# Two float32r products in place of one float32 product for a softmax's sums over partitions

## The chip, the cores and the metric

The kernel runs on one NeuronCore of a Trainium2 chip. The time is the device time of one execution in microseconds (us), taken as the median of several executions. The engines are named as in the profile: PE (TensorE, matrix products; PEld is its loading of the stationary operand), DVE (VectorE), ACT (ScalarE), POOL (GpSimd) and SP (SyncE, which here issues DMAs). They run beside each other, each works through its own queue in order, and they wait for each other by semaphores.

## The reference, cut to what matters

Two attention layers run over eight images of 32 x 32 tokens with 512 channels, each with a group norm before it and a residual after it. The first has 16 heads of 32 channels, the second 4 heads of 128 channels and a relative position term. The second layer's softmax is where the change is:

```
xn     = group_norm(x)
q, k, v = xn @ Wq * scale, xn @ Wk, xn @ Wv        # 4 heads of 128
scores = q @ k + position(q)                       # 1024 x 1024 per head
attn   = exp(scores) / sum over keys of exp(scores)
x      = x + (attn @ v) @ Wo
```

The whole computation is in float32.

## The kernel before, in words

Everything is kept transposed: channels or keys lie on the 128 partitions, tokens along the free dimension. Softmax is taken without subtracting a maximum; a second, general path (which does not run with these inputs) exists for the case that a sum grows too large, so the reciprocals of all sums are put into a tile `checks`.

Each image goes through: load and first norm (`load`), projections of the first layer (`before_0`), first attention (`attention_0`), its output projection (`after_0`), second norm (`norm_1`), projections of the second layer (`second`), second attention (`attention_1`), output projection and store (`after_1`). The function `side_by_side` walks through the steps of one image's `attention_0` and puts beside them pieces of the other parts of the images before and after it, by an account of costs. The projections use seven products where eight would be needed by the plain rule (`seven`, `by_columns` at L299: four products of 32 columns each, side by side in the array).

The steps of `attention_1` have cost 0 in this account, so all 64 of an image come in one unbroken run between two steps of the first attention. I call such a run a burst; there are eight, one per image. In six of them a first attention of a later image still waits to go on.

A burst walks over 4 heads x 2 halves of the queries (a block) x 8 blocks of keys (a step j). A step has

- `front`: two products into one PSUM bank, `ps` = keys x queries in float32 (L631, called QK below) plus the position term in float32r (L632, called pos), and the exponential `e` on ACT (L634);
- `back`, one step behind: the product of the values with `e` into the accumulator `acc` (L643, called AV or acc), and the addition of `e` to `esum` on DVE (L652 for the first pair, L654 for the rest). In the last step of a block ACT copies `acc` out (L657).

After step 1 of the next block comes `finish` for the block that ended: the sum of `esum` over the partitions, as one float32 product with a 128 x 128 matrix of ones (L663, into `su`, in the trace `sums`), and `normalise`: a copy by ACT (L482), a transpose (L484), a reciprocal (L487), the entry in `checks` (L490), a transpose back (L500), all on DVE, and a product with the output on POOL (L504).

Buffers come in rotation by their tags. The PSUM banks have three buffers, which `ps`, `acc` and the sums of the second attention share with the projections and the position term:

```
def bank(name, shape=None):
    return psum.tile(shape or [P, NB], F32, tag="bank", name=name, bufs=3)
```

The tag `e1` has three buffers of 128 x 512 (the exponentials `e`), `es1` two (`esum`), and `rec` two (the copy of the sums and its transpose, for both layers).

The first attention is like the second one with four heads of 32 channels at once: L516 is four products that each use 32 rows of the array (QK0), L524 one exponential of 128 x 2048, L535 four products that each use 32 columns (AV0), L544 and L546 the additions, L556 its sums. In the trace L282 is the last step of a norm (four per image, 128 x 1024 each) and L694 and L240 the load's transposes and statistics; in a burst these belong to a coming image.

The order of instructions on each engine isn't that of the source: a scheduler sets it when the program is built, with a model of its own of how long each instruction takes, and lets an instruction of later work go first where it believes that the engine would wait. Waits are semaphores between engines.

## Time and profile before

| | |
|---|---|
| time, median of 3 | 3999.2 us (3998.8 to 4000.18) |
| profiled execution, span | 3997.9 us |
| busy PE, DVE, ACT, POOL | 3830.9, 2534.3, 1723.6, 579.0 us |
| L663: records, union of busy time | 128 (64 products, two records each), 65.4 us |
| L643, L631, L632: union of busy time | 521.9, 523.6, 406.7 us |

A row of the view in order of time gives the start in us from the span's start, the length, the engine, the line, the operation, what it writes and reads, shape and type, and the number of merged records; in brackets stands the idle time of the engine before it and what ended it. One float32 product gives two records on PE. Records of PE overlap, since a product's record begins before the array is free for it[...]. What a product holds of the array is therefore read from the distance between starts.

### The profile page before, as it was taken

The numbers are of one execution on the slowest core, as the hardware profiler recorded it, in microseconds if no ns is written. First come the engines' busy times: TensorE is split into PE (matmuls) and PEld (weight loads), VectorE is DVE, ScalarE is ACT, GpSimd is POOL, SyncE is SP. The second block draws the span as 40 slices with busy tenths as digits, with TensorE's granted clock in tenths as the row PEclk, the third lists the DMA queues.
The fourth block names the chain that finished last, engine by engine and source line by source line (L and its number), as shares of the span: only waits on it lengthen the run. The fifth ranks groups of instructions, "written<-read, shape, count | busy, mean of one in ns | idle before, by whom it ended". The sixth has DMA issues, their size and how long they took to land. (4 is left out here: it accounts for less than half of the span.)

```text
span 3997.9 us, 71625 instructions
## 1 busy us (share of the span) xinstructions
PE 3830.9 (96%) x30338; PEld 1418.1 (35%) x30338; DVE 2534.3 (63%) x2915; ACT 1723.6 (43%) x1761; POOL 579.0 (14%) x396
## 2 busy tenths in 40 slices
PE   6898999998999989999999989999899998999998
PEld 3232244232443324432244323433234332244353
DVE  5776675576655767458674686646866468664544
ACT  1454453444434444344443445434454444543132
POOL 1340101121111201012100121001110112111101
PEclk9999999999999999999999999999999999999999
DMA  5320120141201512015120241203311032110401
GB/s 145 120 86 25 50 63 6 38 115 58 62 6 38 129 51 60 4 40 143 37 54 12 75 99 38 53 19 93 81 40 45 26 93 60 37 63 10 126 19 22
DMA packets 498694, 234.18 MB, mean 59 GB/s; under 512 B 286368, under 2 KB 478144, under 8 KB 497344
## 3 DMA queue, kind: packets, MB, share of 16 engines
q1 hardware_dynamic: 495232, 214.79, 20.1%
q0 software_dynamic: 2608, 13.70, 0.9%
q8 instruction: 241, 3.95, 0.4%
q10 hardware_dynamic: 528, 1.05, 0.1%
q14 instruction: 85, 0.70, 0.1%
HBM read 170.72 MB, written 58.72 MB: 57 GB/s over the span
## 5 line engine op out<-in xcount | busy, mean ns | idle before, releaser
L524 ACT ACTIVATE e<-ps 128x2048 f32<-128x2048 f32 x512 | 962.0, 1879 | 878.5 <-PE ps L516 723.4
L546 DVE TENSOR_TENSOR es<-es,e 128x2048 f32<-128x2048 f32 x384 | 903.4, 2352 | 450.9 <-ACT e L524 448.0
L516 PE MATMUL ps<-q,k 32*128 32x512 f32 x4096 | 608.0, 649 | 97.3 <-ACT e L524 97.1
L634 ACT ACTIVATE e<-ps 128x512 f32<-128x512 f32 x512 | 305.9, 598 | 583.1 <-PE ps L632 553.0
L535 PE MATMUL acc<-e,v 128*32 128x512 f32 x4096 | 553.9, 613 | 1.4 <-ACT e L524 1.0
L631 PE MATMUL ps<-q,k 128*128 128x512 f32 x1024 | 523.6, 593 | 0.3 <-DVE posT L617 0.3
L643 PE MATMUL acc<-e,v 128*128 128x512 f32 x1024 | 521.9, 592 | 0.0
L654 DVE TENSOR_TENSOR es<-es,e 128x512 f32<-128x512 f32 x384 | 286.9, 747 | 267.1 <-ACT e L634 266.3
L632 PE MATMUL ps<-posT,sel 128*128 128x512 f32 x512 | 406.7, 794 | 0.0
L504 POOL TENSOR_TENSOR q<-q,su 128x512 f32<-128x512 f32 x128 | 201.0, 1571 | 1397.7 <-DVE su L500 1349.6
L516 PEld LDWEIGHTS ps<-q,k 32*128 32x128 f32 x4096 | 165.6, 185 | 500.1 <-issue 250.5
L631 PEld LDWEIGHTS ps<-q,k 128*128 128x128 f32 x1024 | 193.6, 190 | 246.5 <-issue 240.2
L643 PEld LDWEIGHTS acc<-e,v 128*128 128x128 f32 x1024 | 193.1, 189 | 146.8 <-issue 105.2
L535 PEld LDWEIGHTS acc<-e,v 128*32 128x32 f32 x4096 | 81.9, 108 | 394.1 <-issue 348.0
L544 DVE TENSOR_TENSOR es<-e,e 128x2048 f32<-128x2048 f32 x64 | 172.3, 2692 | 36.1 <-ACT e L524 36.1
L484 DVE STREAM_TRANSPOSE tu<-su 128x512 f32<-128x512 f32 x128 | 90.7, 709 | 114.4 <-ACT su L482 114.1
L482 ACT COPY su<-sums 128x512 f32<-128x512 f32 x128 | 75.1, 586 | 171.1 <-PE sums L556 103.3
L632 PEld LDWEIGHTS ps<-posT,sel 128*128 128x128 f32 x512 | 97.3, 190 | 122.5 <-issue 122.5
L652 DVE TENSOR_TENSOR es<-e,e 128x512 f32<-128x512 f32 x64 | 44.9, 701 | 145.5 <-ACT e L634 145.5
L617 DVE TENSOR_TENSOR posT<-pp,posT 32x512 fp32r<-32x512 f32 x128 | 111.7, 873 | 31.7 <-ACT posT L612 30.4
L612 ACT CAST posT<-pp 32x512 fp32r<-32x512 f32 x128 | 105.6, 825 | 46.1 <-PE pp L599 38.0
L408 POOL TENSOR_TENSOR v<-b_v,p_v 128x512 f32<-128x512 f32 x32 | 55.8, 1744 | 479.1 <-ACT p_v L373 458.5
(188 smaller groups left out, 4409.3 us busy)
## 6 DMA issues: line engine op xcount, KB each, us to landing
w_qkv<-ws_qkv SPq DMA_DIRECT2D x168, 128.0 KB, 2.5
xs<-in_x SPq DMA_DIRECT2D x256, 64.0 KB, 2.6
d<-x0T SPq DMA_DIRECT2D x32, 512.0 KB, 3.0
x1T<-d SPq DMA_DIRECT2D x32, 512.0 KB, 6.3
d<-x1T SPq DMA_DIRECT2D x32, 512.0 KB, 3.6
x2T<-d SPq DMA_DIRECT2D x32, 512.0 KB, 6.0
out<-ot SPq DMA_DIRECT2D x256, 64.0 KB, 2.0
w_qkv<-in_L_conv_w_qkv SPq DMA_DIRECT2D x126, 128.0 KB, 2.2
```

What stands on the lines that cost most here:

```text
L504: nc.gpsimd.tensor_tensor(dst, dst, su, op=ALU.mult)
L516: nc.tensor.matmul(ps[:, r, :], k[m][rows, j * P : (j + 1) * P], q[m][rows, h * NB : (h + 1) * NB], start=True, stop=True,)
L524: nc.scalar.activation(e, ps, AF.Exp, scale=D0 ** -0.5)
L535: nc.tensor.matmul(acc[r * D0 : (r + 1) * D0, :], v[:, j, c0 : c0 + D0], e[:, r, :], start=(j == 0), stop=(j == NT - 1),)
L544: nc.vector.tensor_add(state["esum"], state["first"], e)
L546: nc.vector.tensor_add(state["esum"], state["esum"], e)
L617: nc.vector.tensor_sub(rest, logits, greater)
L631: nc.tensor.matmul(ps, k[h][:, keys], q[:, h, queries], start=True, stop=False)
L632: nc.tensor.matmul(ps, sel[:, keys], posT[:, h, queries], start=False, stop=True)
L634: nc.scalar.activation(e, ps, AF.Exp, scale=1.0 / math.sqrt(D1))
L643: nc.tensor.matmul(acc, v[:, j, h * D1 : (h + 1) * D1], e, start=(j == 0), stop=(j == NT - 1),)
L654: nc.vector.tensor_add(state["esum"], state["esum"], e)
```

## The change

The sum over the partitions is no longer one float32 product. `esum` is copied by ACT into a float32r tile (`greater`, in the trace `sg`), which rounds it; DVE subtracts that from `esum` and writes what is left, also as float32r (`rest`, in the trace `sr`). Two float32r products with the ones add both into the same bank. The rest keeps what the rounding takes away, so that the sum stays nearly as exact as in float32, while each product is of the cheaper kind. `greater` takes its buffer from the tag of the exponentials, `rest` from that of the sums' copies. The ones become a float32r tile that is read as float32 elsewhere.

```diff
-    ones = consts.tile([P, P], F32, tag="ones", name="ones")
-    nc.gpsimd.memset(ones, 1.0)
+    ones_r = consts.tile([P, P], F32R, tag="ones", name="ones")
+    nc.gpsimd.memset(ones_r.bitcast(F32), 1.0)
+    ones = ones_r.bitcast(F32)
...
         def finish(h, c, esum):
             name = f"1_{b}_{h}_{c}"
             su = bank(f"sums_{name}")
-            nc.tensor.matmul(su, ones, esum, start=True, stop=True)
+
+            greater = mem.tile([P, NB], F32R, tag="e1", name=f"sg_{name}", bufs=3)
+            nc.scalar.copy(greater, esum)
+            rest = mem.tile([P, NB], F32R, tag="rec", name=f"sr_{name}", bufs=2)
+            nc.vector.tensor_sub(rest, esum, greater.bitcast(F32))
+            nc.tensor.matmul(su, ones_r, greater, start=True, stop=False)
+            nc.tensor.matmul(su, ones_r, rest, start=False, stop=True)
             normalise(q[:, h, c * NB : (c + 1) * NB], su, name)
```

## The prediction

> **What bounds the kernel now.** I read the page's first two parts, then the windows of the second layer's attention, then its instructions in order of time.

> ```profile
> PE 3830.9 (96%) x30338; PEld 1418.1 (35%) x30338; DVE 2534.3 (63%) x2915; ACT 1723.6 (43%) x1761; POOL 579.0 (14%) x396
> PEclk9999999999999999999999999999999999999999
> ```

> TensorE (PE) is busy 96% of the time at full clock. Busy includes pipelining, so I ask where it is really gapless.

> ```profile
> 2057.00:2173.00 116.00, 116.00 (x303) 55.64 (x305) 61.17 (x108) 42.45 (x72) 12.05 (x9) 1.00 0.02 9
> 2173.00:2380.00 207.00, 206.00 (x2010) 63.05 (x2002) 143.21 (x143) 93.60 (x75) 35.62 (x24) 1.00 0.33 86
> ```

> The columns are length, then busy time of PE, PEld, DVE, ACT, POOL. The first window is one "burst", the second layer's attention for one image, eight of which are in the kernel. PE never rests in it, nor in the 207 us after it. So here one us of PE work, or of PE waiting, is one us of the result. The change sits at the end of each of a burst's eight blocks (4 heads, 2 query halves). One such end on each engine:

> ```profile
> 2140.78 1.02 PE L643 MATMUL acc<-e,v 128*128 128x512 f32 x2
> 2141.64 1.02 PE L663 MATMUL sums<-es,ones 128*128 128x512 f32 x2
> 2142.49 1.02 PE L631 MATMUL ps<-q,k 128*128 128x512 f32 x2
> 2142.95 0.80 PE L632 MATMUL ps<-posT,sel 128*128 128x512 f32 x1
> 2143.59 1.02 PE L643 MATMUL acc<-e,v 128*128 128x512 f32 x2
> 2144.44 1.02 PE L631 MATMUL ps<-q,k 128*128 128x512 f32 x2
> ...
> 2140.98 0.60 ACT L634 ACTIVATE e<-ps 128x512 f32<-128x512 f32 x1 [0.50 <-PE ps L632]
> 2142.75 0.59 ACT L482 COPY su<-sums 128x512 f32<-128x512 f32 x1 [1.18 <-PE sums L663]
> 2143.78 0.60 ACT L634 ACTIVATE e<-ps 128x512 f32<-128x512 f32 x1 [0.45 <-PE ps L632]
> ...
> 2141.61 0.69 DVE L652 TENSOR_TENSOR es<-e,e 128x512 f32<-128x512 f32 x1 [3.20 <-ACT e L634]
> 2143.44 0.71 DVE L484 STREAM_TRANSPOSE tu<-su 128x512 f32<-128x512 f32 x1 [1.14 <-ACT su L482]
> ```

> Slots come from starts, not durations. L643 to L663 is 0.86, L663 to L631 0.85: a full float32 product holds the array 0.86 us. L631 to L643, with the float32r product L632 between, is 1.10, so float32r costs 1.10 - 0.86 = 0.24. The su copy (L482) starts 0.26 after the sums' slot ends, an exponential 0.19 after L632's slot ends. Call 2140.78 time 0: before, the third score product (query-key product of key block 3, "QK3") starts at 3.66.

> [...]L299 (32 columns) to L516 (32 rows) takes 1.83 instead of 1.71, and L516 holds 1.07 instead of 0.86:

> ```profile
> 2174.26 1.90 PE L299 MATMUL y_q<-f_xn,w_qkv 128*32 128x512 f32 x16
> 2176.09 1.14 PE L516 MATMUL ps<-q,k 32*128 32x512 f32 x8
> 2177.16 1.07 PE L535 MATMUL acc<-e,v 128*32 128x512 f32 x8
> ```

> [...]

> **Part 1, the product itself.** 64 times, 0.86 becomes 2 x 0.24 = 0.48: -0.38 each, -24 us if nothing waits.

> **Part 2, the copy and the subtraction.** 64 ACT copies (0.59, the row L482) and 64 DVE subtractions (0.69, the row L652). Neither engine is full, so their time as such is free. What matters is where they stand. The changed program's order at an ordinary end is:

> ```
> PE:  acc0, acc1, sums<-greater, QK2, sums<-rest, pos2, [one piece of layer 0], QK3, pos3, acc2
> ACT: e1, greater, su, e2, e3
> DVE: es(e0,e1), rest, tu, es(e2)
> ```

> Before, PE had acc0, sums, QK2, pos2, acc1, QK3. Two things moved. acc1 (which before filled the time before QK3) now stands ahead of the sums, and su now can be made only after the second sums product, which stands behind QK2. QK3 waits for su: there are three banks, one is the running accumulator, one pos2's scores, and the third is the sums' until su has been copied. On ACT the copy su stands ahead of e2.

> Step by step from 0. e1 ends at 0.80 as before, and acc1 wants to start at 0.86; before, this very pair (acc directly after acc, in each burst's last block) took 1.81 instead of 1.71 (the starts 2169.75 and 2171.56), because the exponential came late. So acc1 ends at 1.81. The handover to a 128x128 product is thus some 0.15. greater: 0.83 to 1.42, in time for 1.81. sums<-greater to 2.05, QK2 to 2.90. rest: after es(e0,e1) at 1.52, to 2.21, in time. sums<-rest 2.90 to 3.14, pos2 to 3.38. su: 3.14 + 0.26 = 3.40 to 3.99. QK3: 3.99 + 0.15 = 4.15, where it was 3.66: **+0.49 per end**, the 0.38 gained and more lost in a 0.77 us wait. e2 (4.0 to 4.6) is in time for acc2.

> **Part 3, the pieces of layer 0.** In the six bursts that still have a first-layer attention beside them, the scheduler puts single pieces of it in that gap: four quarters of one QK group (L516) and one AV group (L535) as 1 and 3, then three quarters of the next QK group. A quarter alone holds the array like the whole group. Price from below: 0.86[...]; from above 0.12 + 1.07[...]. From above QK3 stands at 3.38 + 1.19 = 4.57, +0.91. Per burst: four ends with a QK quarter 3.64; the AV quarter (1.0 by L535 before L631[...]) +0.84; the end with three AV parts and a QK quarter (0.12 + 0.88 + 0.12 + 1.07) +1.91; the last block, where a quarter stands ahead of both sums, +0.7. Given back after the burst: one QK and one AV group, 1.19 + 0.88 = 2.07; the second QK group gives nothing, as its fourth quarter still runs alone.

> **Part 4, DVE's queue at the second end.** There the coming image's normalisation runs on DVE:

> ```profile
> 2076.04 1.53 DVE L282 TENSOR_SCALAR x0T<-x0T,back,rstd 128x1024 f32<-128x1024 f32 x2 [1.20 <-POOL rstd L279]
> 2077.49 0.68 DVE L652 TENSOR_TENSOR es<-e,e 128x512 f32<-128x512 f32 x1
> 2078.09 1.53 DVE L282 TENSOR_SCALAR x0T<-x0T,back,rstd 128x1024 f32<-128x1024 f32 x2
> ```

> Time 0 is 2075.05 here (L643). In the new order three L282 (some 0.75 each) stand ahead of es(e0,e1) and rest: 2078.3, then 2078.9, rest done at 2079.53 = 4.48, so sums<-rest starts at 4.63 instead of 2.90. Behind it on PE are pos2 and all that follows: +1.73 more, in six bursts (one L282 stands ahead in the first, but starts later).

> **Sum.** Upper price: six bursts of 3.64 + 0.84 + 1.91 + (0.91 + 1.73) + 0.7 - 2.07 = 7.66 make 46; the two last bursts have 7 plain ends, 14 x 0.49 = 6.9; their last blocks put one of four column groups of a projection between the sums, 2 x 0.86 = 1.7. Together +55: 4054. Lower price: ordinary ends +0.58, 5.2 per burst, 31 + 8.6 = +40: 4039. I take the middle, **4047**[...].

> **Rivals.**
> *A, the arithmetic wins* (faster): nothing waits, -24 us, 3975. For it: PE is the bound and ACT (43%) and DVE (63%) have room. Against it: su's chain of one product, 0.26, 0.59 and 0.15 cannot fit before QK3.
> *B, the pieces are free*: what they hold comes back later. Then 56 x 0.49 + 6 x 1.73 + some 2 - 6 x 2.07 = +27: 4026. Against it: a quarter holds what a group holds.
> *C, worse*: layer 0's exponential (1.88) and addition (2.35), pulled into the burst on ACT and DVE, also hold e3 or es. By my reckoning e3 ends just as acc3 wants it. 1 to 2 us per burst more: 4062.
> *D, no change*: waits of 0.38 eat exactly the gain: 3999. Only if su were some 0.5 earlier.

> **How the numbers follow.** Main case with its two prices 0.63, B 0.20, C 0.08, A 0.05, D 0.04. Range 4020 to 4064: B, main and C are in it, A and D are left out. Faster by over 0.2%: 0.05; within: 0.03; slower: 0.92.

> **What would show it.** In the changed profile, QK1-line products should wait for ACT su, some 0.6 to 0.8 us, at the 14 plain ends; the period of a block should be 16.43 + 0.49 there (before, from the starts of L663: 2158.07 - 2141.64). The second sums product should wait 1.7 us for DVE at the second end of six bursts. The two sums should hold 0.24 each. Single L516 parts should stand in bursts. If QK3 starts without waiting, or the sums' slot isn't 0.24, I am wrong.

## The result, and the profile after

| | before | after |
|---|---|---|
| time, median | 3999.69 us | 4057.12 us |
| ratio after / before, 95% interval | | 1.0143 [1.0126, 1.0161] |
| profiled span | 3997.9 us | 4056.6 us |

The changed kernel is 57.4 us slower; 4047 was predicted, with 4020 to 4064 as the range. From here on lines are those of the changed file: up to L664 they are one higher than before (QK L632, pos L633, AV L644, su L483, QK0 L517), `sg` is L666, `sr` L668, and the two sums products are L669 and L670.

The first lines of the page after, its TensorE row and the clock row:

```profile
PE 3877.3 (96%) x30338; PEld 1425.0 (35%) x30338; DVE 2576.3 (64%) x2979; ACT 1749.8 (43%) x1825; POOL 565.3 (14%) x396
PEclk9999999999999999999999999999999999999999
```

The change takes products away from TensorE, and yet its busy time rose by 46 us. So most of the loss is not idle time. The page before shows 608.0 us for the layer-0 score products, this one 649.2, for the same number of them (part 5 of each page; the first line is of the page before):

```profile
L516 PE MATMUL ps<-q,k 32*128 32x512 f32 x4096 | 608.0, 649 | 97.3 <-ACT e L524 97.1
L517 PE MATMUL ps<-q,k 32*128 32x512 f32 x4096 | 649.2, 650 | 95.7 <-ACT e L525 95.4
L632 PE MATMUL ps<-q,k 128*128 128x512 f32 x1024 | 529.4, 599 | 7.2 <-ACT su L483 6.9
```

Windows over the fourth burst and the stretch behind it, in the columns of the prediction's windows:

```profile
2063.98:2205.37 141.39, 140.43 (x362) 64.54 (x358) 82.95 (x140) 53.20 (x89) 11.60 (x10) 1.00 0.10 24
2205.40:2413.00 207.60, 206.60 (x1999) 63.24 (x2002) 141.91 (x145) 92.97 (x76) 36.62 (x25) 1.00 0.33 90
```

Such a burst took 131.77 us before and takes 141.39 now. The last two, beside which no first-layer attention runs, take 136.3.

**An ordinary end there**, in order of time, on TensorE, ACT and DVE:

```profile
3668.30 1.97 PE L644 MATMUL acc<-e,v 128*128 128x512 f32 x4
3669.71 0.79 PE L669 MATMUL sums<-sg,ones 128*128 128x512 f32 x1
3670.34 1.02 PE L632 MATMUL ps<-q,k 128*128 128x512 f32 x2
3670.80 0.79 PE L670 MATMUL sums<-sr,ones 128*128 128x512 f32 x1
3671.43 0.40 PE L633 MATMUL ps<-posT,sel 128*128 128x512 f32 x1
3672.32 1.12 PE L632 MATMUL ps<-q,k 128*128 128x512 f32 x2 [0.49 <-ACT su L483]
```
```profile
3668.99 0.61 ACT L666 CAST sg<-es 128x512 fp32r<-128x512 f32 x1
3671.68 0.59 ACT L483 COPY su<-sums 128x512 f32<-128x512 f32 x1 [2.08 <-PE sums L670]
```
```profile
3669.13 0.69 DVE L653 TENSOR_TENSOR es<-e,e 128x512 f32<-128x512 f32 x1 [3.20 <-ACT e L635]
3669.74 0.68 DVE L668 TENSOR_TENSOR sr<-es,sg 128x512 fp32r<-128x512 f32 x1
```

Read it by starts. The next block's first two AV products stand together ahead of the sums, `sr` is done at 3670.42, but its product stands behind QK2. `su` can only begin at 3671.68, and QK3 starts 0.05 after its end. Pos2 began at 3671.43 and holds the array 0.24, so TensorE stands still from 3671.67 to 3672.32, 0.65 us (the row's 0.49 is less, since the record of pos2 lasts 0.40). QK3 itself then takes 0.10 longer (1.12 for its two records instead of 1.02).

**The same end in an early burst**: a layer-0 quarter has come into the gap.

```profile
2120.97 0.40 PE L633 MATMUL ps<-posT,sel 128*128 128x512 f32 x1
2121.29 1.12 PE L517 MATMUL ps<-q,k 32*128 32x512 f32 x2
2122.34 1.12 PE L632 MATMUL ps<-q,k 128*128 128x512 f32 x2
```

QK3 is free at 2121.81 (`su` ends there), but starts at 2122.34: the quarter, one product (a pair of records) of the group's four, holds the array 1.05 us, as long as the whole group of the prediction's rows (1.07).

**The second end of such a burst**, with the next image's norm on DVE (TensorE, then DVE):

```profile
2591.87 1.97 PE L644 MATMUL acc<-e,v 128*128 128x512 f32 x4
2593.28 0.79 PE L669 MATMUL sums<-sg,ones 128*128 128x512 f32 x1
2593.91 1.02 PE L632 MATMUL ps<-q,k 128*128 128x512 f32 x2
2595.89 0.50 PE L670 MATMUL sums<-sr,ones 128*128 128x512 f32 x1 [0.96 <-DVE sr L668]
```
```profile
2592.37 2.26 DVE L283 TENSOR_SCALAR x0T<-x0T,back,rstd 128x1024 f32<-128x1024 f32 x3 [1.20 <-POOL rstd L280]
2594.55 0.68 DVE L653 TENSOR_TENSOR es<-e,e 128x512 f32<-128x512 f32 x1
2595.15 0.68 DVE L668 TENSOR_TENSOR sr<-es,sg 128x512 fp32r<-128x512 f32 x1
```

Three norm steps stand ahead of `es` and `sr`; the second product, and all of TensorE behind it, waits for them.

**The account.** I took the period of a block from the start of one sum's first record to that of the next; it was 16.43 us before. It grew by 0.46 at the plain ends, 0.95 at ends with a QK0 quarter, 0.87 with the AV0 quarter, 1.93 with three AV0 parts and a quarter, 2.17 at the second end of bursts 2 to 6 (1.35 in the first). The end of the last block cost 0.86 in six bursts and 1.29 in the last two, by difference. The eight bursts together grew by 8.8 + 5 x 9.62 + 2 x 4.5 = 65.9 us. The first burst began 0.5 later. The six stretches behind the first six bursts became 9.9 shorter (1.64 on average, from 0.6 to 2.5), the one between the last two 2.6 longer, and the end of the span 0.6 shorter. Unrounded, this adds up to 58.6, the difference of the two spans.

### The profile page after: what moved, and what is told of

Its sections match the earlier page's. It is cut to its first block, busy times and chain, and to the rows that moved or that the text cites. A ratio compares the mean times of both kernels' runs of the same rounds, so it can differ in the third digit from the quotient of the medians.

```text
span 4056.6 us, 71579 instructions
## 1 busy us (share of the span) xinstructions
PE 3877.3 (96%) x30338; PEld 1425.0 (35%) x30338; DVE 2576.3 (64%) x2979; ACT 1749.8 (43%) x1825; POOL 565.3 (14%) x396
## 3 DMA queue, kind: packets, MB, share of 16 engines
q10 hardware_dynamic: 528, 1.05, 0.1%
## 4 chain that ended last, share of the span: by engine, by line
PE 88%; DVE 7%; ACT 3%; issue 1%; POOL 1%; DMA 0%; SPq 0%; DVEq 0%; ACTq 0%; POOLq 0%
PE ps L517 14%; PE acc L536 11%; PE ps L632 10%; PE acc L644 10%; PE y_q L300 4%; PE y_k L300 4%; PE y_v L300 4%; PE x_v L300 3%; PE z_k L300 3%; PE ps L633 3%; PE x_q L300 3%; PE z_q L300 3%; PE x_k L300 3%; PE z_v L300 2%; ACT e L525 2%; PE y_wp L300 2%
## 5 line engine op out<-in xcount | busy, mean ns | idle before, releaser
L547 DVE TENSOR_TENSOR es<-es,e 128x2048 f32<-128x2048 f32 x384 | 915.1, 2383 | 453.1 <-ACT e L525 450.0
L517 PE MATMUL ps<-q,k 32*128 32x512 f32 x4096 | 649.2, 650 | 95.7 <-ACT e L525 95.4
L632 PE MATMUL ps<-q,k 128*128 128x512 f32 x1024 | 529.4, 599 | 7.2 <-ACT su L483 6.9
L644 PE MATMUL acc<-e,v 128*128 128x512 f32 x1024 | 518.1, 598 | 0.0
L505 POOL TENSOR_TENSOR q<-q,su 128x512 f32<-128x512 f32 x128 | 191.2, 1494 | 1461.9 <-DVE su L501 1339.0
L633 PE MATMUL ps<-posT,sel 128*128 128x512 f32 x512 | 384.4, 751 | 0.0
L517 PEld LDWEIGHTS ps<-q,k 32*128 32x128 f32 x4096 | 176.4, 185 | 515.3 <-issue 270.1
L632 PEld LDWEIGHTS ps<-q,k 128*128 128x128 f32 x1024 | 188.8, 189 | 253.9 <-issue 204.5
L644 PEld LDWEIGHTS acc<-e,v 128*128 128x128 f32 x1024 | 188.6, 189 | 167.8 <-issue 91.8
L483 ACT COPY su<-sums 128x512 f32<-128x512 f32 x128 | 75.0, 586 | 236.6 <-PE sums L670 132.7
L633 PEld LDWEIGHTS ps<-posT,sel 128*128 128x128 f32 x512 | 97.3, 190 | 121.1 <-issue 121.1
```

What stands on the lines that cost most here:

```text
L505: nc.gpsimd.tensor_tensor(dst, dst, su, op=ALU.mult)
L517: nc.tensor.matmul(ps[:, r, :], k[m][rows, j * P : (j + 1) * P], q[m][rows, h * NB : (h + 1) * NB], start=True, stop=True,)
L547: nc.vector.tensor_add(state["esum"], state["esum"], e)
L632: nc.tensor.matmul(ps, k[h][:, keys], q[:, h, queries], start=True, stop=False)
L633: nc.tensor.matmul(ps, sel[:, keys], posT[:, h, queries], start=False, stop=True)
L644: nc.tensor.matmul(acc, v[:, j, h * D1 : (h + 1) * D1], e, start=(j == 0), stop=(j == NT - 1),)
```

## The experiments

The theory: what costs is the order that the change brings about. The copy `su` comes late behind a second product that stands behind QK2; layer-0 pieces drawn into that gap hold full slots; and at the second end the rest stands in DVE's queue. Rivals: the added work on ACT and DVE costs as such; float32r products, or acc1 ahead of the sums, cost by themselves; the pieces only fill time lost anyway. All diffs are against the changed kernel, and all ratios to the kernel before, run in the same series. The expected times start from 3999.7 us for the kernel before; beside these runs it took 4001.4 to 4002.6, so a time near the edge of a range says less than the ratio and the periods.

**1. Copy and subtraction without their use.** The sum is the old product; `greater` and `rest` go nowhere.

```diff
-            nc.tensor.matmul(su, ones_r, greater, start=True, stop=False)
-            nc.tensor.matmul(su, ones_r, rest, start=False, stop=True)
+            nc.tensor.matmul(su, ones, esum, start=True, stop=True)
```

> The copy to float32r and the subtraction are made as in the change, but the sum is taken by the one float32 product of before, so their results go nowhere. TensorE's order is exactly that of before. Theory (the order and the waits cost, the added work as such is hidden): 3998 to 4003 us. Rival (ACT's and DVE's added work itself is what costs, as 64 copies of 0.6 us and 64 subtractions of 0.7 us hold exponentials or additions back): 4020 us or more.

Measured: ratio 1.0 [0.9991, 1.0008]; no block's period differs from before by more than 0.004 us. In this order the 64 copies and 64 subtractions on ACT and DVE are free. The first rival falls.

**2. Only the greater part's product.**

```diff
-            rest = mem.tile([P, NB], F32R, tag="rec", name=f"sr_{name}", bufs=2)
-            nc.vector.tensor_sub(rest, esum, greater.bitcast(F32))
-            nc.tensor.matmul(su, ones_r, greater, start=True, stop=False)
-            nc.tensor.matmul(su, ones_r, rest, start=False, stop=True)
+            nc.tensor.matmul(su, ones_r, greater, start=True, stop=True)
```

> Only the first product: the rests are left out of the sum. The sums' bank is complete 1.1 us earlier in a block's end, acc1 still stands ahead of the sum as in the change, and no piece of layer 0 stands in the ordinary ends. Theory (QK3 waits for su because the second product comes late): su is copied by 3.05, pos2 ends at 3.14, so no wait; each of 56 ends gains 0.50 to 0.62 us against before (16.43 becomes 15.8 to 15.9), the second ends lose up to 0.9 to e2's buffer, six last blocks have one layer-0 piece: 3964 to 3978 us. Rival (acc1 ahead of the sums, or float32r products that hold more than 0.24 us here, cost by themselves): 4000 us or more.

Measured: ratio 0.9926 [0.9909, 0.9943], 3971.9 us; nearly every end is 0.53 to 0.54 us shorter. TensorE at an ordinary end:

```profile
3612.69 1.98 PE L644 MATMUL acc<-e,v 128*128 128x512 f32 x4
3614.10 0.79 PE L667 MATMUL sums<-sg,ones 128*128 128x512 f32 x1
3614.73 1.02 PE L632 MATMUL ps<-q,k 128*128 128x512 f32 x2
3615.19 0.80 PE L633 MATMUL ps<-posT,sel 128*128 128x512 f32 x1
3615.82 1.02 PE L632 MATMUL ps<-q,k 128*128 128x512 f32 x2
```

acc1 still stands ahead of the sum, yet QK3 starts 3.13 after acc0 without a wait (4.02 in the changed kernel). Replacing 0.86 by 0.24 should save 0.62; 0.53 was saved, so by difference acc1's place costs 0.09. The second ends, where no rest stands in DVE's queue now, lost nothing, though up to 0.9 was allowed for them.

**3. No layer-0 piece in a burst.** For two steps of the first attention after each burst, its products are kept in program order.

```diff
+                if after_burst[0]:
+                    tc.keep_in_program_order(ins)
...
+        after_burst[0] = 2
```

> The change, with the layer-0 groups after each burst kept in program order, so that none of their parts stands in a burst; the order at an ordinary end is else the change's. Theory (each piece costs a full slot, partly in the place of the wait, and gives back about 1.5 us per burst later): all ordinary ends have a period of 16.43 + 0.46 = 16.89, the second ends some 18.1, so bursts grow by about 4.6 instead of 9.6 us; 4032 to 4042 us. Rival (pieces only fill time that is lost to the wait anyway and come back in full): 4054 to 4062 us.

Measured: ratio 1.0111 [1.0094, 1.0128], 4046 us. The time lies between the two theories, nearer to the first, but the periods are as it had them: all ordinary ends now +0.46, in every burst, with a wait for `su` at each of the 56 ends inside the bursts (the waits of TensorE):

```profile
PE ps L639 <- ACT su L483: 27.6, 56, 0.5
```

Bursts 2 to 6 grow by 5.5 instead of 9.6 us. All bursts together grow by 41.2 instead of 65.9, so the pieces held 24.7 us, of which the changed kernel got 9.9 back behind its bursts. The time also holds what has nothing to do with pieces: the first burst began 3.4 us earlier than before (3.5 in run 2, where no order was kept), and the six stretches between bursts grew by 3.7 us. Both are, by my estimate, about what phases of half clock account for (see the last section), so the periods are the clean measure.

**4. Parts made early**, in `back`, as soon as the last addition is done, and handed to `finish`.

```diff
+            greater = mem.tile([P, NB], F32R, tag="e1", name=f"sg_{name}", bufs=3)
+            nc.scalar.copy(greater, state["esum"])
+            rest = mem.tile([P, NB], F32R, tag="rec", name=f"sr_{name}", bufs=2)
+            nc.vector.tensor_sub(rest, state["esum"], greater.bitcast(F32))
             nc.scalar.copy(q[:, h, c * NB : (c + 1) * NB], acc)
-            state["ended"] = (h, c, state["esum"])
+            state["ended"] = (h, c, (greater, rest))
```

> Greater parts and rests are made as soon as the last addition is done, ahead of the accumulator's copy, so that both products stand together where the one float32 product stood; TensorE's order at ordinary ends is that of before. Theory: sg 0.6 us after e0, done before acc1's exponential starts; su is then ready 1.1 us before QK3; each ordinary end gains 0.38 us (16.43 becomes 16.05). At the second ends of six bursts the additions of e0 and e1 stand behind three normalisations and the rest on DVE, and e2 wants e0's buffer: up to 1 us lost there; a layer-0 piece in six last blocks: 3978 to 3992 us. Rival (float32r halves cost as much as the float32 product, or the extra work on ACT holds e1): 4000 us or more.

Measured: ratio 0.9978 [0.9969, 0.9988], 3993.4 us, 1.4 above the expected range. TensorE and ACT:

```profile
3613.05 1.02 PE L644 MATMUL acc<-e,v 128*128 128x512 f32 x2
3613.51 0.80 PE L670 MATMUL sums<-sg,ones 128*128 128x512 f32 x1
3614.14 0.40 PE L671 MATMUL sums<-sr,ones 128*128 128x512 f32 x1
3614.38 1.02 PE L632 MATMUL ps<-q,k 128*128 128x512 f32 x2
```
```profile
3611.30 0.60 ACT L635 ACTIVATE e<-ps 128x512 f32<-128x512 f32 x1 [1.35 <-PE ps L633]
3611.79 0.61 ACT L659 CAST sg<-es 128x512 fp32r<-128x512 f32 x1
```

The ordinary ends gain 0.385 each, the arithmetic's 0.38: acc0 at 3613.05, its slot of 0.86, two slots of 0.24, QK2 at 3614.38. (Behind a float32 product, a float32r record begins with that product's second record, so its start, 3613.51 here, 0.46 after that product's, is not its slot; behind another float32r product, as at 3614.14, it is.) The same two products that cost 0.46 in the changed order gain 0.385 here. The 1 us that I allowed at second ends was not lost (in bursts 2 to 6 the second and third ends together miss 0.1; in the first burst 1.2 was lost, see run 5), but the last blocks cost 1.16 in six bursts, where a QK0 quarter stands ahead of the late parts.

**5. One word: the buffer of the greater part.**

```diff
-            greater = mem.tile([P, NB], F32R, tag="e1", name=f"sg_{name}", bufs=3)
+            greater = mem.tile([P, NB], F32R, tag="rec", name=f"sg_{name}", bufs=2)
```

> The change with one word altered: the greater parts lie in a buffer of the tag rec instead of e1. The exponentials' ring of three then no longer makes the copy follow the next block's second exponential: in the built program it stands ahead of the next block's first one, and TensorE has the order of before with both products in the old sum's place. Theory (the change loses through the order that the place of the copy brings about): ordinary ends 16.43 - 0.385 = 16.05 us; second ends 0 to 0.4 less than before; in the last blocks the parts come late and one layer-0 piece (or one column group) stands ahead, +1.16 in six and +0.42 in two, as in the run with early parts: 3986 to 3994 us. Rival (extra copies, subtractions and products cost in any order): 4040 us or more.

Measured: ratio 0.9991 [0.9983, 1.0], 3998.4 us: slower than expected, but the whole loss of 57 us is gone. Built so, the order at ordinary ends is again acc0, sums, QK2, pos2, acc1, and these gain 0.385. So the order, and not the products, made the change slow, and the ring of `e1`, for a copy made at this place of the program, made the order: in it the copy followed the next block's second exponential. The miss lies around the third block's start in bursts 2 to 6, where one new wait appears (waits, then ACT, then DVE):

```profile
PE acc L644 <- ACT e L635: 5.0, 5, 1.0
```
```profile
2085.12 0.60 ACT L635 ACTIVATE e<-ps 128x512 f32<-128x512 f32 x1 [1.35 <-PE ps L633]
2088.81 0.62 ACT L666 CAST sg<-es 128x512 fp32r<-128x512 f32 x1 [3.10 <-DVE es L655]
2089.34 0.59 ACT L635 ACTIVATE e<-ps 128x512 f32<-128x512 f32 x1
```
```profile
2086.11 1.21 DVE L323 TENSOR_TENSOR f_xn<-x0T,f_xn 128x1024 f32<-128x1024 f32 x1
2087.25 1.47 DVE L655 TENSOR_TENSOR es<-es,e 128x512 f32<-128x512 f32 x2
```

Now the copy stands ahead of the next block's first exponential on ACT. When DVE's last additions are late behind the load's work, the copy waits, the exponential behind it waits with it, and TensorE for that. By the 0.19 us that an exponential starts after its scores elsewhere, this one could, as an estimate, have started at 2087.06, while the copy waited, but it started at 2089.34, behind the copy: ACT kept its order here, and that costs TensorE 1.0 us five times. In the first burst the same late copy holds the accumulator's copy behind it on ACT, and with it the sums' product: one wait of 1.3 us (`PE sums L669 <- ACT q L658`). Runs 4, 6, 9 and 10 have one wait of 1.0 to 1.2 at the same place.

**6. Rest in `es1`, greater part in `rec`, old product in the last block.**

```diff
+            if (h, c) == (H1 - 1, NH - 1):
+                nc.tensor.matmul(su, ones, esum, start=True, stop=True)
+                normalise(q[:, h, c * NB : (c + 1) * NB], su, name)
+                return
```

> Greater parts in the tag rec, rests in the tag es1, and the last block of each burst keeps the one float32 product of before, so that no piece and no wait stands there. Theory: 56 ends gain 0.385 us each, the eight last blocks are those of before: 3999.7 - 21.6 = 3978, in 3974 to 3984 us. Rival (what is gained at the ends is lost later, in the first layer's attention or in waits for weights): 3990 to 4000 us.

Measured: ratio 0.9975 [0.9965, 0.9985], 3992 us: in the rival's range. The bursts together shorten by 14.8 us instead of 21.6. Those without a load shorten by 2.7 us each, as 7 x 0.385 has it, those with a load by 1.6 (the first by 1.3). The rest is the wait of run 5 (0.73 longer, not 0.385 shorter, in the period that holds it). Between the bursts 4.3 us are lost, 2.4 of them between the last two (see the last section).

**7. The second block's rest on GpSimd.**

```diff
+            if (h, c) == (0, 1):
+                nc.gpsimd.tensor_tensor(rest, esum, greater.bitcast(F32), op=ALU.subtract)
+            else:
+                nc.vector.tensor_sub(rest, esum, greater.bitcast(F32))
```

> The change, with the rest of each burst's second block (head 0, second query half) made by GpSimd instead of DVE, all else as in the change but that both products stand together at that end. GpSimd takes some 1.4 us for such an operation (its rows of 128x512). Theory (three normalisations ahead of the rest on DVE hold the second end): the rest comes at 3.0 instead of 4.5 us, QK3 at 4.3 to 4.4, so second ends grow by 0.7 to 0.9 instead of 2.17 us: 4046 to 4052 us. Rival (these ends are long for another reason, such as the layer-0 piece or ACT): growth still about 2 us, 4054 to 4060 us.

Measured: ratio 1.0119 [1.0103, 1.0134], 4050.1 us. The second ends grow by 0.99 instead of 2.17 us, near the theory's 0.7 to 0.9 and far from 2; GpSimd took 1.56 for one on average. At that end the products also stand together and no piece is there, so not all of the 1.18 is DVE's queue; run 3, where the order is the change's, has +1.46 there against +0.46 elsewhere, and so puts the queue at 1.0.

**8. Rest in `es1`.** The greater part stays in `e1`, acc1 ahead of the sums.

```diff
-            rest = mem.tile([P, NB], F32R, tag="rec", name=f"sr_{name}", bufs=2)
+            rest = mem.tile([P, NB], F32R, tag="es1", name=f"sr_{name}", bufs=2)
```

> The change with the rest in a buffer of the tag es1 instead of rec; the greater part stays in e1. In the built program acc1 still stands ahead of the sums, but at 49 of 56 ends both products stand together ahead of QK2 and no layer-0 piece is there; seven ends (one per early burst, two in the first) keep the changed order with a piece. Theory (what is lost is su's chain behind a second product that follows QK2, not acc1's place nor the products): sums<-rest ends at 2.44, su at 3.29, so QK3 starts after pos2 at 3.54, which is 0.1 less than before: these ends have 16.3 to 16.4 us instead of 16.89; the whole 4000 to 4012 us. Rival (acc1's place or the parts themselves cost): these ends stay at 16.8 or more, 4025 us or more.

Measured: ratio 1.0049 [1.0034, 1.0064], 4020.5 us. The 49 ends behave as the theory has it, even better: 0.15 shorter than before. TensorE there:

```profile
3654.80 0.51 PE L670 MATMUL sums<-sr,ones 128*128 128x512 f32 x1
3655.14 1.02 PE L632 MATMUL ps<-q,k 128*128 128x512 f32 x2
3655.59 0.80 PE L633 MATMUL ps<-posT,sel 128*128 128x512 f32 x1
3656.23 1.02 PE L632 MATMUL ps<-q,k 128*128 128x512 f32 x2
```

With the second product ahead of QK2 instead of behind it, `su` is in time and QK3 follows pos2. Against +0.46, that one exchange is worth 0.61 per end. The total lies between theory and rival: the second ends, still in the changed order with a piece and with the wait for DVE, cost 2.06 (3.74 in the second burst, where 1.7 more go to a phase of half clock), and 6.0 us were lost between the bursts.

**9. Old product also in the second block**, as run 6 but with the condition `(h, c) == (H1 - 1, NH - 1) or (h, c) == (0, 1)`.

> As the run with the last block's old product, and the second block of each burst (head 0, second query half) also keeps the one float32 product, so that no rest stands in DVE's queue beside the coming image's normalisation. Theory: the second ends are those of before (0 instead of +0.73, and +1.35 in the first burst), 48 ends gain 0.39 each: bursts shorten by 18.7 us; 2 to 3 us are given back in a half-clock phase after the wait for w_q between the last two bursts, as in the other runs: ratio to before 0.9955 to 0.9965, 3983 to 3988 us where before takes 4000. Rival (the lost time at the second ends has another cause): no better than the run before it, ratio 0.9975.

Measured: ratio 0.997 [0.9959, 0.9981], 3989.7 us, hardly distinguishable from run 6. My reason for the loss was wrong in its place: a wait is left at the *third* end, where the copy again stands ahead of an exponential and waits for the last additions (acc0 there starts 0.22 us late), and the first burst keeps 1.5 us, of which a wait of 1.2 for the same late exponential is the most.

**10. Parts early (run 4) and the old product in the last block.** There the copy stands behind the next block's first exponential, and at second ends the rest stands behind the norm's small operations, while these wait for GpSimd.

```diff
+            if (h, c) == (H1 - 1, NH - 1):
+                nc.scalar.copy(q[:, h, c * NB : (c + 1) * NB], acc)
+                state["ended"] = (h, c, (None, state["esum"]))
+                return
             greater = mem.tile([P, NB], F32R, tag="e1", name=f"sg_{name}", bufs=3)
...
+            if greater is None:
+                nc.tensor.matmul(su, ones, rest, start=True, stop=True)
+            else:
```

> Parts made early as in that run (greater in e1, rest in rec), and the last block of each burst keeps the one float32 product of before. Theory (the second ends are lost where DVE makes the rest in the midst of the coming image's normalisation; with early parts it stands after that chain's last small operation, while the chain waits for GpSimd anyway, and the second and third ends together lost only 0.1 us there): bursts 2 to 6 shorten by 1.77 + 1.16 - 0.01 = 2.9 us each, the last two by 2.7, the first by 1.7: 21.8 in all; less 2 to 3 us in the half-clock phase between the last two bursts: ratio to before 0.9945 to 0.996. Rival (what the ends gain is given back between bursts): ratio 0.997 or more.

Measured: ratio 0.9963 [0.9949, 0.9976], 3986.4 us beside 4001.4 for before. Of the versions that compute the sum in full it has the lowest ratio, 15 us below before and some 70 below the changed kernel, though its interval overlaps that of run 9. Its ratio lies between theory and rival. The bursts shorten by 19.9 us of the 21.8 that I had (2.6 instead of 2.9 in bursts 2 to 6), and the profiled span by 15.9: 2.8 are lost between the last two bursts and 3.3 in the six stretches before, so a part is given back, as in the other runs. The last section has what takes it.

## Why the prediction was right, point by point

- **The bound.** Right. TensorE's order and waits at the ends make the 65.9 us of the bursts; runs 1 and 4 leave ACT's and DVE's added work as such at nothing.
- **Part 1**, 0.38 per sum: right to the digit in runs 4, 5, 6 and 10 (0.385), and none of it is to be had in the order that the change got.
- **Part 2**, +0.49 at plain ends: measured +0.46 to +0.47. `su` was to begin at 3.40 and began 3.38 after acc0 (3671.68 - 3668.30). QK3 was to start at 4.15 and started at 4.02; the other 0.10 came in QK3 itself. So the wait is 0.65, not 0.77, and the handover of 0.15 is 0.05 ahead of the start and 0.10 behind it. Runs 2 and 8 show the cause.
- **Part 3**, the pieces. The upper price was right nearly everywhere: QK0 quarter 0.91 predicted, 0.95 measured; AV0 quarter 0.84 and 0.87; the triple end 1.91 and 1.93; last block 0.7 and 0.86. What failed is the choice between the prices: "I take the middle"; nothing measured stood behind it. The lower price had 0.86 for a quarter alone, which held 1.05 at the early end above, and none of the difference is hidden by the wait: `su` was free 0.53 us before the quarter left the array, so what the quarter holds longer is added in full. That is 7 us of what is missing at 4047 (10 by the times, 11 by the spans). The term given back was 2.07 per burst, and the stretches became only 1.64 shorter on average, 2.6 us less in all. But the pieces do give back what was priced: by the estimate of the last section 2.03 to 2.12 in run 7. What the prediction put at nothing is the clock: more of TensorE's work between the bursts fell into phases of half clock, and such a phase came in between the last two bursts (2.6 us). Bursts 1 us shorter than the upper price stand against that.
- **Part 4**, DVE's queue: right in kind, too large in size. +1.73 was predicted over an ordinary end, 2.17 - 0.95 = 1.22 came, and 0.4 in the first burst. The first norm step starts 0.50 after acc0 (2592.37 - 2591.87), while I took it from the trace of before at 0.99: the stretched first end delays TensorE by 0.95, and DVE's norm only by 0.46 (from the burst's start, 35.29 before and 35.75 after). That the sum of 9.73 per burst stood all the same (9.62) is luck: this term was 0.5 too large, and the last block and the other ends 0.4 too small. The last two bursts grew by 4.5 instead of 4.3, their last blocks by 1.29 instead of 0.86.
- **Rivals.** A (3975) fails on the order alone: in another order the arithmetic does win, though 15 us and not 24 (run 10). B (4026) fails, since of the 24.7 us that the pieces held about half came back at most. D (3999) fails at the plain ends, which lose 0.46 with no piece there. C expected 1 to 2 us more per burst from layer 0's exponentials and additions; the bursts grew no more than the main case's upper price, so nothing of that was seen, though 4062 is near the time.

## What to carry to other kernels

Moving work to engines with room pays only if the product that uses it comes no later (an ordinary end gained 0.385 us in run 4 and lost 0.46 in the changed kernel): place the second half of a split product beside the first, ahead of the long work, and see what its bank's next user waits for. Which buffer ring a new tile is put in can set its place in an engine's queue, and with it the whole order; in this kernel one tag was worth some 60 us. When the scheduler fills a gap with a piece of another group, price the piece by what it holds (here 1.05 us for a quarter, 1.07 for the whole group), not by its share of the work.

## What the runs showed of the hardware

In the six stretches behind the first six bursts, such phases stand around a wait of TensorE of 7.8 to 8.1 us before and 6.5 to 8.2 after. The wait that ends, and a window within the phase, before and then after (the granted clock is the third number from the right):

```profile
1908.69 2.09 PE L516 MATMUL ps<-q,k 32*128 32x512 f32 x8 [8.14 <-ACT e L524]
1905.51:1912.30 6.79, 3.61 (x16) 0.91 (x20) 5.63 (x4) 3.27 (x2) 0.00 (x0) 0.50 0.00 0
```
```profile
1930.62 2.09 PE L517 MATMUL ps<-q,k 32*128 32x512 f32 x8 [6.49 <-ACT e L525]
1926.60:1936.80 10.20, 6.18 (x28) 1.51 (x32) 8.52 (x5) 3.76 (x2) 0.00 (x0) 0.50 0.01 2
```

How much of TensorE's work a phase catches changes with where the grid falls: 3.61 us in the window of before, 6.18 in the one of after. I count half of TensorE's busy time in it as lost, which is an estimate. In run 7 the first five stretches are 1.55 to 1.68 us shorter than before, with 0.90 to 0.98 us more work at half clock in each; without that the pieces give back 2.03 to 2.12, where the prediction had 2.07. Runs 3, 4, 6 and 10 grew by 1.9 to 4.8 us in the six stretches, and the estimate gives 2.0 to 5.5 for them; in runs 5, 8 and 9 it leaves 1 to 2 us open.

Between the last two bursts TensorE waits for a weight transfer, 3.01 us before and 3.84 after. The wait and what follows it, before and then after, then the windows behind each wait:

```profile
3750.58 1.92 PE L299 MATMUL x_q<-x1T,w_q 128*32 128x512 f32 x16 [3.01 <-DMA w_q<-in_L_conv_Wq]
```
```profile
3803.50 3.27 PE L300 MATMUL x_q<-x1T,w_q 128*32 128x512 f32 x16 [3.84 <-DMA w_q<-in_L_conv_Wq]
```
```profile
3750.60:3754.00 3.40, 3.40 (x32) 1.23 (x36) 0.00 (x0) 0.59 (x1) 0.00 (x0) 1.00 0.86 242
```
```profile
3804.00:3807.20 3.20, 3.20 (x20) 1.00 (x16) 0.00 (x0) 0.38 (x1) 0.00 (x0) 0.50 0.86 233
```

After the longer wait the clock is halved for 3.4 us: four records, one from each of four products side by side, take 0.85 instead of 0.43. The longer wait (0.8) and the slow phase (1.7) make the 2.6 us lost there. In every run but the first experiment, which waited 3.0 us as before, this phase appeared, behind waits of 3.1 to 4.2 us, and the stretch between the two bursts was 1.7 to 3.0 us longer than before.

The length of the wait alone does not decide it. In the kernel before the grid cuts the wait of 3.01 us so that no step holds more than 1.9 us of it, and the clock stays at 1.00. In the changed kernel the step from 3800.52 holds 3.0 us of the wait, and the clock is 0.50 from the end of that step, 3803.93, on. So a step need not be idle throughout: in run 6 about 2.4 us lay in the step ahead of the slow phase (by the granted clock of 0.52 in the window 3741.20 to 3744.30). Nor does the idle time within one step decide it: beside the first layer's products of the changed kernel TensorE was idle for 1.0 us in the step ahead of 1916.36, and a phase began there, while the step from 1919.77 on held 1.0 us too, and the clock stayed at 1.00 behind it. In run 7 the wait was 3.1 us, hardly longer than before, and the stretch still became 1.7 longer.
